# Queries and keys of a second attention, transposed in blocks by VectorE and moved through DRAM, with projections four units ahead

## The chip, the cores and the metric

The kernel runs on one core of a Trainium2 chip. The core has a matrix engine (TensorE, PE in the profile), a vector engine (VectorE, DVE), a scalar engine (ScalarE, ACT), a general engine (GpSimd, POOL) and a queue engine that only issues transfers (SyncE, SP). On-chip data lies in SBUF, 128 partitions wide; products land in PSUM. Transfers run on 16 DMA engines. The metric is the device time of one execution in microseconds, the median over runs.

## The reference

All numbers are float32. Eight sequences of 128 tokens and 512 channels pass through two residual blocks:

```
x = x + attention1(x @ cond_w[adapter])          # 32 heads of 16, causal
h = attention2(x, cached keys and values)        # 32 query heads and 8 key heads of 128
x = x + h @ kernel + bias + LoRA(h)
```

The second attention is where the change lies:

```
q = rope(rmsnorm(x @ Wq.T))                      # 32 heads of 128
k = rope(rmsnorm(x @ Wk.T)); v = x @ Wv.T        # 8 heads of 128, each serves 4 query heads
keys = concat(k_cache[block_table], k)           # 512 cached positions and 128 own
vals = concat(v_cache[block_table], v)
scores = q . keys / sqrt(128), masked by length
h = softmax(scores) . vals, then @ Wo.T
```

## The kernel before

**Units and pairs.** The second attention is cut into 64 units, each one key head g and one sequence b: 128 queries of four heads against 640 keys. Two units of the same sequence and neighbouring key heads are a pair, since one row of the gathered cache holds both heads. The order is written out by hand (a manual schedule): each engine executes its instructions in program order.

**One iteration u** of the loop over units does, on TensorE: the scores of unit u, head by head (L889 against the 512 cached keys, L896 against the 128 own keys), with the query projection of unit u+1 between the heads (L177, qp); the key and value projection of u+1 (L217, kvp); the weighted values of unit u-1 (L963); the transposes of the queries of u+1 (`queries`, L254); the output projection of u-1 (L982, yp); and the transpose of the own keys of u+1 (`own_keys`, L271). ScalarE copies both transposes out of PSUM (L256, L273). A float32 product is two weight loads and two product instructions, so each line counts twice in the profile; a transpose is one.

**Softmax.** VectorE adds mask and scores, scales and takes the maximum in one instruction for each head (L902), ScalarE takes the exponential (L912) and divides (L880, after a reciprocal on VectorE, L879). The probabilities are transposed in 32 x 32 blocks by VectorE (`turn`, L883, into `flips`, of which there is one buffer) and sixteen DMAs of 80 KB each (L936) put the blocks in place, from `flips` to `pT`. The product with the values of an iteration later reads `pT`.

**Cached keys.** From unit 4 on, they are transposed the same way: `turn_keys` (L840, four block transposes for each pair) writes `flk`, and `move_keys` (L853) issues sixteen DMAs for each pair, eight in each of two iterations, from `flk` to `kT`. `pair_keys` calls these at the third head of an iteration. For units 0 to 3 TensorE transposes them (`keys`, L263).

**Projections.** `q_turn` multiplies the projected queries with tables of cosine and sine, weighted by the norm's weights (VectorE, L200 to L202), and GpSimd adds the halves (L203). The tables `ca` and `sa` lie in SBUF for the whole kernel. `kv_turn` does the same for the keys (L232 to L235), `norms` takes the reciprocal roots (GpSimd, L244) and scales the keys (L247).

**Buffers and queues.** Scores have two PSUM tiles (`p_sc`), projections and outputs two (`p_mm`), transposes and kvp two (`p_tp`). SBUF tiles of 2 KB per partition come from a ring `tile_a` of twelve slots, which the gathered weights of the first attention (cw) and the LoRA weights (la, lb, las, lbs, gs) share. SP issues nearly all DMAs in program order[...]. GpSimd issues the gathers (kg, vg, cw).

**The first attention** runs before, in 17 steps k of half a sequence; `gather_w`, `condition` (L514), `merge_loads` (L425 to L433) and `merge_gates` (L447) lie in it.

Of the kernel before, what the change touches and what calls it, by code (L numbers as in the profile page):

```python
# [41 lines left out]
def block_kernel(  # L42
# [47 lines left out]
    def tile_a(shape, name):  # L90
        return both.tile(shape, F32, tag="a", name=name, bufs=12)

# [16 lines left out]

    ca = [one([P, B, D2], F32, f"ca_{n}") for n in range(2)]  # L110
    sa = [one([P, B, D2], F32, f"sa_{n}") for n in range(2)]
    bias = one([P, DM], F32, "bias")
# [8 lines left out]

    oT_kept = one([P, REP, S], F32, "oT_kept")

    weights = {}
# [60 lines left out]
    def q_turn(u):  # L185

        b = units[u][1]
        s = st[u]
        qp = s["qp"]

        def table(t, cols):
            return t[:, b, cols].unsqueeze(1).to_broadcast([P, REP, cols.stop - cols.start])

        s["ss"] = both.tile([P, REP + 1], F32, tag="ss", name=f"ss_{u}")
        sq = tile_a([P, REP, D2], f"sq_{u}")
        qa = s["qa"] = tile_a([P, REP, D2], f"qa_{u}")
        qb = tile_a([P, REP, D2], f"qb_{u}")

        def turn():
            nc.vector.tensor_tensor(qa[:], qp[:], table(ca[0], slice(0, D2)), ALU.mult)  # L200
            nc.vector.tensor_tensor(qb[:, :, lo], qp[:, :, hi], table(sa[0], lo), ALU.mult)
            nc.vector.tensor_tensor(qb[:, :, hi], qp[:, :, lo], table(sa[0], hi), ALU.mult)  # L202
            nc.gpsimd.tensor_tensor(qa[:], qa[:], qb[:], ALU.add)  # L203
            nc.scalar.activation(sq[:], qp[:], AF.Square)

        def squares():
            nc.vector.tensor_reduce(s["ss"][:, :REP], sq[:], AX.X, ALU.add)

        return turn, squares
# [11 lines left out]
    def kv_turn(u):  # L221

        b = units[u][1]
        s = st[u]
        kp, ss = s["kp"], s["ss"]
        junk = both.tile([P, D2], F32, tag="junk", name=f"junk_{u}", bufs=1)
        nc.scalar.activation(junk[:], kp[:, :D2], AF.Square, accum_out=ss[:, REP:])
        vo = both.tile([P, D2], F32, tag="vo", name=f"vo_{u}", bufs=3)
        nc.scalar.copy(vo[:], kp[:, D2:])
        ka = both.tile([P, D2], F32, tag="ka", name=f"ka_{u}")  # L230
        kb = both.tile([P, D2], F32, tag="kb", name=f"kb_{u}")
        nc.vector.tensor_tensor(ka[:], kp[:, :D2], ca[1][:, b, :], ALU.mult)  # L232
        nc.vector.tensor_tensor(kb[:, lo], kp[:, hi], sa[1][:, b, lo], ALU.mult)
        nc.vector.tensor_tensor(kb[:, hi], kp[:, lo], sa[1][:, b, hi], ALU.mult)
        nc.gpsimd.tensor_tensor(ka[:], ka[:], kb[:], ALU.add)  # L235
        s |= {"ka": ka, "vo": vo}

    def norms(u):
        s = st[u]
        ss, ka = s["ss"], s["ka"]  # L240

        nc.vector.tensor_scalar(ss[:], ss[:], 1.0 / D2, EPS, ALU.mult, ALU.add)  # L242
        rs = both.tile([P, REP + 1], F32, tag="rs", name=f"rs_{u}")
        nc.gpsimd.tensor_tensor(rs[:], ss[:], minus_half[:], ALU.pow)  # L244
        nq = both.tile([P, REP], F32, tag="nq", name=f"nq_{u}", bufs=3)
        nc.vector.tensor_scalar(nq[:], rs[:, :REP], -SCALE2, None, ALU.mult)
        nc.vector.tensor_scalar(ka[:], ka[:], rs[:, REP:], None, ALU.mult)  # L247
        s["nq"] = nq

    def queries(u):  # L250
        s = st[u]
        tp = p_tp.tile([P, REP, S], F32, tag="tp", name=f"qTp_{u}")
        for r in range(REP):
            nc.tensor.transpose(tp[:, r, :], s["qa"][:, r, :], ident[:])  # L254
        s["qT"] = tile_a([P, REP, S], f"qT_{u}")
        nc.scalar.copy(s["qT"][:], tp[:])  # L256

    def keys(u):
# [6 lines left out]
        nc.scalar.copy(kT[:].rearrange("p k j -> p (k j)"), tp[:].rearrange("p c k -> p (c k)"))  # L265
        s["kT"] = kT[:]

    def own_keys(u):
        s = st[u]
        tp = p_tp.tile([P, S], F32, tag="tp", name=f"kTp_{u}")  # L270
        nc.tensor.transpose(tp[:], s["ka"][:], ident[:])  # L271
        s["kTo"] = both.tile([P, S], F32, tag="kTo", name=f"kTo_{u}")
        nc.scalar.copy(s["kTo"][:], tp[:])  # L273


    with (
# [68 lines left out]
        nc.vector.tensor_copy(row_f[:], row[:])  # L345
        ahead = both.tile([P, 4, P], I32, tag="a", name="ahead", bufs=12)
        nc.gpsimd.iota(ahead[:], pattern=[[-32, 4], [1, P]], base=0, channel_multiplier=0)
# [40 lines left out]
        def angles():  # L388
# [19 lines left out]
            return (fr, trig["sin"]), (kf, trig["cos"])  # L408

        def tables(n):  # L410
            for here, there in ((lo, hi), (hi, lo)):
                w_here = wn[n][:, here].unsqueeze(1).to_broadcast([P, B, HALF])
                w_there = wn[n][:, there].unsqueeze(1).to_broadcast([P, B, HALF])
                nc.gpsimd.tensor_tensor(ca[n][:, :, here], trig["cos"], w_here, ALU.mult)
                nc.gpsimd.tensor_tensor(sa[n][:, :, here], trig["sin"], w_there, ALU.mult)
            nc.gpsimd.tensor_scalar(sa[n][:, :, lo], sa[n][:, :, lo], -1.0, None, ALU.mult)

        merge = {}

        def merge_loads():  # L420
# [7 lines left out]
            for key, src in (("las", lora_as), ("lbs", lora_bs)):  # L428
                merge[key] = tile_a([RANK, DM], key)
                nc.sync.dma_start(out=merge[key][:], in_=src)  # L430
# [7 lines left out]
        def merge_gates():  # L438
# [4 lines left out]
            )  # L443
            gs = [tile_a([P, 2, B * RANK], f"gs_{n}") for n in range(2)]
            merge["gs"] = [gs[c // 2][:, c % 2, :] for c in range(4)]
# [255 lines left out]
        for k in range(2 * B + 1):  # L701
# [45 lines left out]
            else:  # L747
# [36 lines left out]
                elif b == 2:  # L784
                    tables(1)
                    nc.gpsimd.memset(minus_half[:], -0.5)
                elif b == 3:
# [45 lines left out]

    def turn_keys(n):


        flk = p2.tile([P, 4, NBLK, 2, 32], F32, tag="flk", name=f"flk_{n}", bufs=1)
        for h, half in enumerate(pairs[n]["kg"]):
            for m in range(2):
                nc.vector.transpose(  # L840
                    flk[:, :, 2 * h : 2 * h + 2, m, :].rearrange("p b c i -> p c b i"),
                    half[:, :, m, :],
                )
        pairs[n]["flk"] = flk
        kT = p2.tile([P, NBLK, 4, 2, 32], F32, tag="kT2", name=f"kT2_{n}")
        pairs[n]["kT"] = kT
        for m in range(2):
            st[2 * n + m]["kT"] = kT[:, :, :, m, :].rearrange("p c a i -> p (c a) i")

    def move_keys(n, a):  # L850

        for b in range(4):
            nc.sync.dma_start(  # L853
                out=pairs[n]["kT"][32 * b : 32 * b + 32, :, a].rearrange("p c m i -> p c (m i)"),
                in_=pairs[n]["flk"][32 * a : 32 * a + 32, b].rearrange("p c m i -> p c (m i)"),
            )

    def pair_keys(u):

        if u == 2:  # L860
            turn_keys(u)
        if 1 < u < N - 2:
            for a in range(u % 2 * 2, u % 2 * 2 + 2):
                move_keys(u // 2 + 1, a)

    def scores(u, between, after):
# [20 lines left out]
        for r in range(REP):  # L887
            sc = p_sc.tile([P, 1024], F32, tag="sc", name=f"sc_{u}_{r}")
            nc.tensor.matmul(  # L889
                sc[:, : NBLK * P].rearrange("p (k j) -> p k j", j=32),  # L890
                s["qT"][:, r, :],
                s["kT"],
# [3 lines left out]
            nc.tensor.matmul(  # L896
                sc[:, NBLK * P : NK], s["qT"][:, r, :], s["kTo"][:], start=True, stop=True
            )
# [153 lines left out]
    for u in range(N + 1):  # L1052


        now, nxt, last = u < N, u + 1 < N, 1 <= u <= N

        def between(r):
            if nxt:
                for c in ((), (0,), (1,), (2, 3))[r]:
                    q_matmul(u + 1, c)  # L1060
                if r == REP - 1:
                    after[:] = q_turn(u + 1)

        after = [lambda: None] * 2
        if now:
            scores(u, between, after)
        if nxt:
            for c in range(KC):
                kv_matmul(u + 1, c)
            kv_turn(u + 1)  # L1070
            after[1]()
# [7 lines left out]
        if u == 0:  # L1079
            x1_last = out_proj_last()  # L1080
        if nxt:
            norms(u + 1)
            queries(u + 1)
            for v in {0: (1,), 1: (2, 3)}.get(u, ()):
                keys(v)
            if u > 2 and u % 2 and u // 2 + 2 < N // 2:
                turn_keys(u // 2 + 2)

            if u < 2:
                gather(u + 1, "kg")  # L1090
            elif u % 2 == 0:
                gather(u // 2 + 2, "kg")
            if u % 2:
                gather(u // 2 + 1, "vg")
        if u == N:
# [5 lines left out]
        if u == N - 1:  # L1101
            flips_last(u, (2, 3))
        if u == 0:
            flip_last(x1_last)
        if nxt:
            own_keys(u + 1)
        if u == 0:
            load_wo(1)

        for n in range(2):  # L1110
            g = (u + 1 - n) // (2 * B) * 2 + 2 + n
            if (u + 1 - n) % (2 * B) == 2 * B - 2 and g < NKV:
                load_qkv(g)
# [88 lines left out]
```

## Time and profile before

| | |
|---|---|
| median of 3 runs | 1414.28 us (1413.05 to 1415.44) |
| profiled execution | 1423.96 us, span 1421.1 us |
| clock of TensorE granted | 0.997 of full speed |
| first attention | 0 to about 220 us |
| one unit of the second attention | 17.8 us |
| DMA moved | 180.26 MB, mean 127 GB/s |

In lines of the profile a group shows its line of code, its engine, what it writes and reads, how often, then busy time in all, mean duration of one in ns, and after the last bar the time the engine idled before it and for whom. In lines of the timeline the first column is the start and the second the duration in us; in brackets stands the idle time before. In the chain of waits a piece is start, duration and what ran. The main groups of the second attention beside the ones shown in the prediction:

| line | what | count | mean ns |
|---|---|---|---|
| L889 | scores, 512 keys | 512 | 593 |
| L896 | scores, own keys | 512 | 275 |
| L254 | transposes of queries | 256 | 273 |
| L271 | transposes of own keys | 64 | 273 |
| L902 | mask, scale, maximum | 256 | 884 |
| L883 | block transposes of probabilities, 640 columns | 252 | 808 |
| L840 | block transposes of cached keys, 256 columns | 120 | 413 |
| L207 | sum of squares, 512 values to 4 | 64 | 665 |
| L627 | sums in the first attention, 1024 values to 8 | 32 | 1200 |

These durations include the pipeline's length: one product ends after the next has begun, so they add up to more than the time that passes.

### The profile page before, as it was taken

The numbers are of one execution on the slowest core, as the hardware profiler recorded it, in microseconds if no ns is written. First come the engines' busy times: TensorE is split into PE (matmuls) and PEld (weight loads), VectorE is DVE, ScalarE is ACT, GpSimd is POOL, SyncE is SP. The second block draws the span as 40 slices with busy tenths as digits, with TensorE's granted clock in tenths as the row PEclk, the third lists the DMA queues.
The fourth block names the chain that finished last, engine by engine and source line by source line (L and its number), as shares of the span: only waits on it lengthen the run. The fifth ranks groups of instructions, "written<-read, shape, count | busy, mean of one in ns | idle before, by whom it ended". The sixth has DMA issues, their size and how long they took to land.

```text
span 1421.1 us, 20290 instructions
## 1 busy us (share of the span) xinstructions
PE 1391.5 (98%) x6244; PEld 898.5 (63%) x6244; DVE 931.8 (66%) x2266; ACT 655.9 (46%) x1520; POOL 568.2 (40%) x553
## 2 busy tenths in 40 slices
PE   6999989999999999999999999999999999999998
PEld 6877755566666666666666666666666665666555
DVE  5777846566666666666666666666666665666651
ACT  3555535444444444444444444444444444344431
POOL 5774342433333333333333333333333433343220
PEclk9999999999999999999999999999999999999999
DMA  6255013444444565444445654444456544444440
GB/s 198 75 164 183 31 37 104 129 117 118 119 115 119 161 193 151 119 119 119 119 119 159 196 148 119 118 119 119 121 160 192 152 117 136 131 111 112 115 111 30
DMA packets 156202, 180.26 MB, mean 127 GB/s; under 512 B 92416, under 2 KB 97792, under 8 KB 156096
## 3 DMA queue, kind: packets, MB, share of 16 engines
q1 hardware_dynamic: 140544, 134.39, 34.0%
q0 software_dynamic: 15552, 44.58, 10.8%
q8 instruction: 50, 0.82, 0.2%
q14 instruction: 56, 0.46, 0.1%
HBM read 75.83 MB, written 4.72 MB: 57 GB/s over the span
## 4 chain that ended last, share of the span: by engine, by line
PE 93%; DVE 2%; issue 2%; DMA 1%; ACT 1%; POOL 1%; SPq 1%; another core or an unknown queue 0%; DVEq 0%; POOLq 0%; ACTq 0%
PE op L963 19%; PE qp L177 15%; PE sc L889 15%; PE yp L982 15%; PE kvp L217 7%; PE sc L896 4%; PE fp L1044 2%; PE hp L514 2%; PE qTp L254 2%; PE pT1p L638 2%; PE qp L530 2%; PE att L673 2%; PE o L657 1%; PE sc L595 1%; PE kvp L545 1%
## 5 line engine op out<-in xcount | busy, mean ns | idle before, releaser
L902 DVE CUSTOM_DVE_ANT_0 pr<-sc,mask,nq 128x640 f32<-128x640 f32 x256 | 226.0, 884 | 144.2 <-PE sc L896 90.9
L912 ACT ACTIVATE pr<-pr,nm 128x640 f32<-128x640 f32 x256 | 211.8, 827 | 189.3 <-DVE nm L902 102.1
L889 PE MATMUL sc<-kT,qT 128*128 128x512 f32 x512 | 262.0, 593 | 0.0
L177 PE MATMUL qp<-wq,x1T 128*128 128x512 f32 x512 | 251.2, 593 | 0.0
L963 PE MATMUL op<-pT,vg 128*128 128x256 f32 x1024 | 242.0, 379 | 1.6 <-DMA pT<-fl 1.6
L203 POOL TENSOR_TENSOR qa<-qa,qb 128x512 f32<-128x512 f32 x64 | 81.8, 1278 | 375.2 <-DVE sums L879 375.2
L982 PE MATMUL yp<-wo,oT 128*128 128x512 f32 x504 | 229.2, 598 | 2.0 <-DVE oT L971 2.0
L963 PEld LDWEIGHTS op<-pT,vg 128*128 128x128 f32 x1024 | 193.9, 190 | 27.8 <-DVE sums L879 1.8
L880 ACT ACTIVATE pr<-pr,sums 128x640 f32<-128x640 f32 x256 | 208.4, 814 | 0.0
L883 DVE STREAM_TRANSPOSE fl<-pr 128x640 f32<-128x640 f32 x252 | 189.2, 808 | 0.0
L896 PEld LDWEIGHTS sc<-kTo,qT 128*128 128x128 f32 x512 | 96.4, 190 | 124.4 <-issue 119.2
L982 PEld LDWEIGHTS yp<-wo,oT 128*128 128x128 f32 x504 | 91.4, 191 | 95.1 <-issue 91.5
L160 POOL DMA_INDIRECT kg<-in_k_cache_dram,idx_kv x128 | 131.6, 1029 | 35.3 <-issue 34.8
L160 POOL DMA_INDIRECT vg<-in_v_cache_dram,idx_kv x128 | 128.6, 1005 | 37.8 <-issue 33.6
L889 PEld LDWEIGHTS sc<-kT,qT 128*128 128x128 f32 x512 | 87.7, 191 | 80.2 <-issue 77.8
L256 ACT COPY qT<-qTp 128x512 f32<-128x512 f32 x64 | 37.5, 586 | 205.3 <-PE qTp L254 204.7
L217 PEld LDWEIGHTS kvp<-wkv,x1T 128*128 128x128 f32 x512 | 97.3, 190 | 40.5 <-issue 30.1
L217 PE MATMUL kvp<-wkv,x1T 128*128 128x256 f32 x512 | 121.0, 379 | 0.0
L244 POOL TENSOR_TENSOR rs<-ss,minus_half 128x5 f32<-128x5 f32 x64 | 76.5, 1196 | 83.1 <-DVE ss L242 82.2
L177 PEld LDWEIGHTS qp<-wq,x1T 128*128 128x128 f32 x512 | 82.8, 191 | 31.5 <-issue 31.5
L896 PE MATMUL sc<-kTo,qT 128*128 128x128 f32 x512 | 99.2, 275 | 0.0
L273 ACT COPY kTo<-kTp 128x128 f32<-128x128 f32 x64 | 17.1, 267 | 166.4 <-issue 115.2
(155 smaller groups left out, 1701.1 us busy)
## 6 DMA issues: line engine op xcount, KB each, us to landing
pT<-fl SPq DMA_DIRECT2D x1008, 80.0 KB
kT<-flk SPq DMA_DIRECT2D x480, 32.0 KB
wq<-in_wq_dram SPq DMA_DIRECT2D x8, 1024.0 KB
wo<-in_wo_dram SPq DMA_DIRECT2D x8, 1024.0 KB
wkv<-in_wkv_dram SPq DMA_DIRECT2D x8, 512.0 KB
kg<-in_k_cache_dram,idx_kv POOLq DMA_INDIRECT x128
vg<-in_v_cache_dram,idx_kv POOLq DMA_INDIRECT x128
res<-x_kept SPq DMA_DIRECT2D x8, 256.0 KB
```

Source lines behind the costliest of these rows:

```text
L160: nc.gpsimd.indirect_dma_start(out=dst[:, c].rearrange("p n d -> p (n d)"), out_offset=None, in_=src, in_offset=bass.IndirectOffsetOnAxis( ...
L177: nc.tensor.matmul(s["qp"][:].rearrange("p h d -> p (h d)"), x1T[b][:, c, :], weights[g][0][:, c, :], start=(c == 0), stop=(c == KC - 1),)
L203: nc.gpsimd.tensor_tensor(qa[:], qa[:], qb[:], ALU.add)
L217: nc.tensor.matmul(s["kp"][:], x1T[b][:, c, :], weights[g][1][:, c, :], start=(c == 0), stop=(c == KC - 1))
L880: nc.scalar.activation(prs[r][:], prs[r][:], AF.Copy, scale=sums[:, r : r + 1])
L883: nc.vector.transpose(s["flips"][:, :, :, r, :].rearrange("p b c j -> p c b j"), prs[r][:])
L889: nc.tensor.matmul(sc[:, : NBLK * P].rearrange("p (k j) -> p k j", j=32), s["qT"][:, r, :], s["kT"], start=True, stop=True,)
L896: nc.tensor.matmul(sc[:, NBLK * P : NK], s["qT"][:, r, :], s["kTo"][:], start=True, stop=True)
L902: nc.vector.tensor_tensor_reduce(out=pr[:], in0=sc[:, :NK], in1=mask[:], scale=s["nq"][:, r : r + 1], scalar=3.0e38, op0=ALU.add, op1=ALU.min,
L912: nc.scalar.activation(pr[:], pr[:], AF.Exp, bias=nm[:, r : r + 1], scale=-1.0, accum_out=sums[:, r : r + 1],)
L963: nc.tensor.matmul(ops[h][:, : 2 * S], cached(u, "vg", c) if c < NBLK else s["vo"][:], s["pT"][:, :, c, 2 * h : 2 * h + 2, :].rearrange("p ...
L982: nc.tensor.matmul(yp[:], s["oT"][:, r, :], weights[g][2][:, r, :], start=(r == 0), stop=(r == REP - 1))
```

## The change

From unit 4 on, TensorE transposes neither queries nor own keys. `turn_ahead` block-transposes both on VectorE, the queries into `flq` and the own keys into a fifth block of `flk`. For each pair, `keys_out` writes `flk` and `flq` to DRAM in two DMAs, and an iteration later `keys_in` reads them into `kT` and `qT` in eight, with the blocks in place. One head's query matrix is then `qT[:, a, i, r, m]` at fixed r and m. To leave time for this, a unit is projected four iterations ahead rather than one; iterations 0 and 1 project the units in between. Units 1 to 3 keep the transposes on TensorE. To make room, the tables go to DRAM and are loaded for each pair (`load_tab`), `tile_a` has nine slots rather than twelve, and las, lbs and gs have tiles of their own; ka, vo and nq have more buffers.

```diff
-        return both.tile(shape, F32, tag="a", name=name, bufs=12)
+        return both.tile(shape, F32, tag="a", name=name, bufs=9)
...
-    ca = [one([P, B, D2], F32, f"ca_{n}") for n in range(2)]
-    sa = [one([P, B, D2], F32, f"sa_{n}") for n in range(2)]
+    tab_kept = dram.tile([B, P, 4, D2], F32, tag="tab", name="tab_kept")
+    tabs = {}
...
+    def load_tab(n):
+        if n < N // 2:
+            tabs[n] = both.tile([P, 4, D2], F32, tag="tab", name=f"tab_{n}")
+            nc.sync.dma_start(out=tabs[n][:], in_=tab_kept[n % B])
...
     def turn_keys(n):
-        flk = p2.tile([P, 4, NBLK, 2, 32], F32, tag="flk", name=f"flk_{n}", bufs=1)
+        flk = p2.tile([P, 4, 2, NBLK + 1, 32], F32, tag="flk", name=f"flk_{n}", bufs=1)
...
+        kT = p2.tile([P, 4, 2, NBLK + 1, 32], F32, tag="kT2", name=f"kT2_{n}")
+        pairs[n]["fl"] = [flk, p2.tile([P, 4, 32, REP, 2], F32, tag="flq", name=f"flq_{n}", bufs=1)]
+        qT = p2.tile([P, 4, 32, REP, 2], F32, tag="qT2", name=f"qT2_{n}")
+        pairs[n]["to"] = [kT, qT]
         for m in range(2):
+            s = st[2 * n + m]
+            s["kT"] = kT[:, :, m, :NBLK].rearrange("p a c i -> p c a i")
+            s["qT"] = [
+                qT[:, :, :, r].rearrange("p a i m -> p (a i) m")[:, :, m] for r in range(REP)
+            ]
+            s["kTo"] = kT[:, :, m, NBLK]
+
+    def turn_ahead(v):
+        (flk, flq), m = pairs[v // 2]["fl"], v % 2
+        nc.vector.transpose(
+            flq[:, :, :, :, m].rearrange("p b i r -> p r b i"),
+            st[v]["qa"][:].rearrange("p r d -> p (r d)"),
+        )
+        nc.vector.transpose(flk[:, :, m, NBLK], st[v]["ka"][:])
+
+    def keys_out(n):
+        pairs[n]["dr"] = []
+        for k, fl in enumerate(pairs[n]["fl"]):
+            kept = dram.tile([P, 4, 320 - 64 * k], F32, tag=f"fl{k}", name=f"kept{k}_{n}", bufs=2)
+            nc.sync.dma_start(out=kept[:], in_=fl[:].rearrange(FLAT[k]))
+            pairs[n]["dr"].append(kept)
+
+    def keys_in(n):
+        for k, to in enumerate(pairs[n]["to"]):
+            kept = pairs[n]["dr"][k][:].rearrange("(a j) b x -> j b a x", j=32)
+            for b in range(4):
+                nc.sync.dma_start(
+                    out=to[32 * b : 32 * b + 32].rearrange(FLAT[k]),
+                    in_=kept[:, b],
+                )
 
     def pair_keys(u):
         if u == 2:
-            turn_keys(u)
+            turn_keys(2)
+            turn_ahead(4)
         if 1 < u < N - 2:
-            for a in range(u % 2 * 2, u % 2 * 2 + 2):
-                move_keys(u // 2 + 1, a)
+            if u % 2 == 0:
+                turn_ahead(u + 3)
+                keys_out(u // 2 + 1)
+            else:
+                keys_in(u // 2 + 1)
...
-        now, nxt, last = u < N, u + 1 < N, 1 <= u <= N
+        now, last = u < N, 1 <= u <= N
+        ahead = {0: [1, 2, 3], 1: [4, 5]}.get(u, [u + 4] if u + 4 < N else [])
...
-        if nxt:
-            norms(u + 1)
-            queries(u + 1)
...
+        if ahead:
+            norms(ahead[0])
+        if u == 0:
+            queries(1)
+            keys(1)
+        if u == 1:
+            keys(2)
+            keys(3)
+        if u > 2 and u % 2 and u // 2 + 2 < N // 2:
+            turn_keys(u // 2 + 2)
+            turn_ahead(u + 3)
...
         if u == 0:
+            project(2)
             flip_last(x1_last)
-        if nxt:
-            own_keys(u + 1)
-        if u == 0:
+            own_keys(1)
+            norms(2)
+            project(3)
+            queries(2)
+            own_keys(2)
+            norms(3)
+            load_tab(2)
+            load_tab(3)
             load_wo(1)
+        elif u == 1:
+            queries(3)
+            own_keys(3)
+            project(5)
+            norms(5)
+        if u % 2:
+            load_tab((u + 7) // 2)
 
         for n in range(2):
-            g = (u + 1 - n) // (2 * B) * 2 + 2 + n
-            if (u + 1 - n) % (2 * B) == 2 * B - 2 and g < NKV:
+            g = (u + 4 - n) // (2 * B) * 2 + 2 + n
+            if (u + 4 - n) % (2 * B) == 2 * B - 2 and g < NKV:
                 load_qkv(g)
```

## The prediction

> **What bounds the kernel.** I read the engine table first, then the chain of waits, then one unit's pieces of it.
>
> ```profile
> PE 1391.5 (98%) x6244; PEld 898.5 (63%) x6244; DVE 931.8 (66%) x2266; ACT 655.9 (46%) x1520; POOL 568.2 (40%) x553
> PE 93%; DVE 2%; issue 2%; DMA 1%; ACT 1%; POOL 1%; SPq 1%; another core or an unknown queue 0%; DVEq 0%; POOLq 0%; ACTq 0%
> 309.67 0.44 PE qTp L254 x4
> 310.11 3.44 PE yp L982 x8
> 313.55 0.11 PE kTp L271
> 313.65 0.86 PE sc L889 x2
> 314.51 0.22 PE sc L896 x2
> 314.74 0.86 PE sc L889 x2
> ```
>
> TensorE works without a gap, and the chain is its own instruction stream: columns are start, duration, line. A unit takes 17.78 us (kTp at 313.55, again at 331.33). The pieces show the pace, not the pipelined ends: a product of 512 columns holds the engine for 0.43 us, one of 128 for 0.11, that is 0.84 ns a column. So an instruction taken from TensorE is time, if nothing else then ends last.
>
> **What leaves TensorE.** The change drops L254 (four transposes, 0.44 us) and L271 (one, 0.11) for units 4 to 63: 60 x 0.55 = **-33 us**. ScalarE loses their two copies (586 and 267 ns), which were not in the chain.
>
> **The new layout of the queries.** qT was contiguous. Now one head's query is read from [a, i, r, m] with r and m innermost: 8 floats, 32 bytes, from one column to the next. It is the stationary operand. Weight loads overlap products (PEld), so a slower load costs only where the product before it is short. Per head the order is load, product of 512, twice, then load, product of 128, twice. A contiguous load is 128 columns, 0.11 us at that pace, and just fits behind a product of 128. Strided loads behind such a product: the second L896 of each head (4), and the first L889 of head 1, which has no qp between. Five per unit; the others hide behind 0.43 us.
>
> No load in the trace has such a stride. The nearest rows are two VectorE reductions of the same 128 values, one read in runs of 16, one at 128 bytes a step:
>
> ```profile
> L334 DVE TENSOR_REDUCE eye_f<-ident 128x32 f32<-128x128 f32 x1 | 0.4, 361 | 0.0
> L318 DVE TENSOR_REDUCE odd<-ident 128x2 f32<-128x128 f32 x1 | 0.3, 286 | 0.4 <-POOL ident masks.py:199 0.4
> ```
>
> The step adds 75 ns over 128 values (L334 also writes 30 more results, which may be part of it). Against the contiguous rate of L207 and L627, (1200 - 665) ns for 512 values, 128 values would be some 264 ns, and 97 is added. [...] By the rows, 0.09: 60 x 5 x 0.09 = **+27 us**. [...] A gain is excluded, since the contiguous load is hidden. I take 27.
>
> The moving operands keep runs of 32 floats, as kT had at 593 ns a product like any contiguous one: nothing.
>
> **VectorE.** turn_ahead adds two transposes a unit. By L883 (640 in steps of 0.75 us) 512 columns are 0.60 and 128 are 0.17: 0.8 us, if writes at 32 bytes are no slower; 1.1 by the reading rate above. In even units they stand before the fourth L902, where VectorE idles 0.97 us: hidden. In odd units they stand behind turn_keys:
>
> ```profile
> 828.35 0.34 DVE L247 TENSOR_SCALAR ka<-ka,rs 128x128 f32<-128x128 f32 x1
> 828.74 1.42 DVE L840 STREAM_TRANSPOSE flk<-kg 128x256 f32<-128x256 f32 x4
> 830.26 0.69 DVE L989 TENSOR_TENSOR y<-yp,y 128x512 f32<-128x512 f32 x1
> 830.87 0.55 DVE L874 TENSOR_SCALAR mask<-place,lens_f 128x640 f32<-128x640 f32 x1
> 831.56 0.88 DVE L902 CUSTOM_DVE_ANT_0 pr<-sc,mask,nq 128x640 f32<-128x640 f32 x1
> ```
>
> Behind them wait y, the mask and the first L902, and for its end waits TensorE: scores have two PSUM buffers, so head 2 needs head 0's freed. Today it is free at 832.44 and wanted at 833.19. After: L840 ends at 830.16, both transposes at 830.9, y and mask take 1.3, L902 ends near 833.05; TensorE, rid of 0.55, wants it at 832.63. It stalls 0.5 us, once a pair, 29 pairs: 14.5 us. But the loads delay TensorE too, three of the five before head 2 (0.27): 0.22 remains, **+6 us**.
>
> **The last units.** Projections run four units ahead, so iterations 60 to 62 have none; before, only 63. Without 5.1 us of qp and kvp the values (L963) come sooner than their probabilities:
>
> ```profile
> 1374.22 10.25 SPq L936 DMA_DIRECT2D pT<-fl  x16
> 1386.44 1.97 PE L963 MATMUL op<-pT,vg 128*128 128x256 f32 x8 [1.57 <-DMA pT<-fl]
> ```
>
> Sixteen issues take 10.25 us and the wait ends 1.97 after them: 12.2 from the transposed probabilities to use. Today 63 waits 1.57. In a full unit the transposes end about 12.2 us after the first L889 and the values start 9.5 into the next unit, leaving some 2.5 us. Scores alone take 4.6. Running 60 to 63 by this: waits of 2.4, 1.7 (an FFN tail lies in it), 0 and 4.2 = 8.3, less 1.57: **+7 us**. The projections themselves are moved to iterations 0 and 1, not saved; each brings its turn (VectorE 2.9 us, POOL's L203, L235 and L244, 2.9 us) in the same order among itself, under 5.1 us of its own products. At the start TensorE waits 1.06 us for own_keys(1) today; there a projection stands before each of queries(2) and own_keys(2), so I put no gain and no loss (1 us either way). The load of the next wq and wkv moves three units earlier with them, still behind pT's issues at the end of an iteration, two iterations before its first use as before.
>
> **Transfers.** Per pair sixteen kT<-flk of 32 KB (0.5 MB) become two writes and eight reads, 1.18 MB each way, plus a table load of 256 KB. pT's thirty-two stay. SP's issues fall from 48 to 43 a pair; the same eight-issue slot (5.2 to 6.8 us, L853) takes the reads. The stretches 804 to 832 us show the DMA engines at 0.36 to 0.83, 247 GB/s at 0.83; 6.3 MB in 34.5 us is 180 GB/s, so they fit. Reads issued at 817 to 823 land near 826, wanted at 829.6: hidden. The cover goes where SP issues weights just before them: wq and wkv (1.5 MB, 6 us) three times, wo (1 MB) three times. I count 3 x 1 to 2.5 and 3 x 0 to 0.7: **+5 us** (0 to 10). The write to DRAM must land before its reads issue; a whole unit lies between. keys_out adds a wait of SP for turn_ahead at the third head; behind it on SP stand this unit's pT, whose own transposes come later on the same VectorE, so nobody waits longer. The table load waits for a kv_turn of the same iteration, long over by then; q_turn reads it three iterations later.
>
> **The first attention.** Nine tile_a slots instead of twelve: lb_1 now reuses a slot of cw_7, so it waits for condition(7), which ends at 156; las waited for that before (issued at 155.41). Behind it on SP stand lb_2, lb_3, w_eff, las, lbs and gc, 1.75 MB, and VectorE's gs (L447, at 161.57) needs gc, now near 165. VectorE stalls and the copies L644 and sums behind it come late: **+3 us** (0 to 4). tab_kept (2 MB) holds SP near 93 us, where nothing behind it is due soon: 0; with no cover, its 9 us. In unit 2 two turn_aheads more precede L902 of head 3; TensorE waits there 2.0 us for oT already, 2 x 0.8 comes on top: **+1.5 us**.
>
> **Sum.** -33 + 27 + 6 + 7 + 5 + 3 + 1.5 = +16.5 us. The profiled execution took 1424.0 (span 1421.1), 10 more than the median 1414.3; so 1440 there and **1431** in the runs, slower by 1.2%. Its own range is 1418 to 1450.
>
> **Rivals.**
>
> *The strided load is free* (decides if the load stays below 0.11 us). Then the stall of VectorE is whole: -33 + 14.5 + 7 + 5 + 3 + 1.5 = -2: **1412**. With the other costs at their lower ends (0.25 a pair, 4 in the tail, no load collisions, no gc) it is -21: 1393. For it: fp32 runs at half the rate a 2-byte load shows (L583's loads 95 ns against L530's 192), so there may be room. Against it: the reductions[...].
>
> [...]
>
> *The transfers end last*: doubled bytes put the keys' reads or pT 1 us late in every pair, since pT has only 2.5 us to spare and fl is one buffer that waits for its reads. On top of the forecast 30 us: **1461**. For it: 1.3 MB of pT follow 1.2 MB of keys in the same queue. Against: the busy shares.
>
> **Chances.** Forecast 0.50, load free 0.30[...], transfers 0.12. Changes under 0.2% (2.8 us) can't be told from none. Of the free load two thirds are faster by more, the rest within or above; of the forecast a tenth falls low. Faster 0.26, same 0.09, slower 0.65. The range 1395 to 1464 leaves out [...]the best of the free load.
>
> **What would show it.** PEld's rows for L889 and L896 (191 and 190 ns now) near 280 if the load pays, unchanged if not; the chain's L896 pairs at 0.31 instead of 0.22; L902 of head 0 releasing TensorE at odd-to-even seams; waits on pT in the last three units; no wait on kT or qT reads but after weights. The forecast is wrong if L896 keeps 0.22, or if waits on transfers exceed 20 us in all.

## The result

The changed kernel takes **1453.22 us** (median of 6 runs, 1450.07 to 1453.96), the kernel before 1414.86 us on the same chip (6 runs, 1413.05 to 1416.27). The ratio is **1.0269** (95% interval 1.0256 to 1.0283): slower by 38 us. The forecast was slower by 16.5: the sign and the places are right, the size is not.

The profile of the changed kernel, by its engine table, the first line of its chain of waits and three of its groups, and below them the two load groups of the kernel before:

```profile
PE 1407.8 (97%) x5944; PEld 985.4 (68%) x5944; DVE 992.2 (68%) x2386; ACT 603.1 (42%) x1400; POOL 555.5 (38%) x553
PE 85%; DMA 4%; DVE 4%; SPq 3%; ACT 1%; issue 1%; POOL 1%; DVEq 0%; ACTq 0%; POOLq 0%
L938 PE MATMUL sc<-kT,qT 128*128 128x512 f32 x512 | 276.8, 622 | 13.4 <-DMA pT<-fl 6.9
L938 PEld LDWEIGHTS sc<-kT,qT 128*128 128x128 f32 x512 | 151.3, 314 | 89.6 <-issue 49.8
L945 PEld LDWEIGHTS sc<-kT,qT 128*128 128x128 f32 x480 | 150.3, 313 | 55.3
```

```profile
L889 PEld LDWEIGHTS sc<-kT,qT 128*128 128x128 f32 x512 | 87.7, 191 | 80.2 <-issue 77.8
L896 PEld LDWEIGHTS sc<-kTo,qT 128*128 128x128 f32 x512 | 96.4, 190 | 124.4 <-issue 119.2
```

L938 and L945 are the old L889 and L896, the scores. TensorE is busy for 97% of the span, with 300 instructions fewer and for 16 us longer; its share of the chain has fallen from 93 to 85%. The loads of its stationary operand show the main reason: 314 and 313 ns each, where they took 191 and 190. One unit's start in the chain of waits (start, duration, what ran):

```profile
840.47 0.86 PE sc L938 x2
841.33 0.35 PE sc L945 x2
841.67 0.99 PE sc L938 x2
842.66 0.34 PE sc L945 x2
843.00 0.86 PE qp L183 x2
843.86 0.86 PE sc L938 x2
844.72 0.34 PE sc L945 x2
```

A pair of 128 columns took 0.22 us before and takes 0.34; head 1's pair of 512 took 0.86 and takes 0.99, head 0's still 0.86. These are the five places that the prediction named, and no others. A unit now pays 4 x 0.12 + 0.13 = 0.61 us to save 0.55.

The second cost is at the seam from an odd to an even unit. The timeline there (start, duration, engine, line; idle time before in brackets):

```profile
820.83 1.41 DVE L862 STREAM_TRANSPOSE flk<-kg 128x256 f32<-128x256 f32 x4
822.17 1.06 DVE L881 STREAM_TRANSPOSE flq<-qa 128x512 f32<-128x512 f32 x1
823.09 0.26 DVE L885 STREAM_TRANSPOSE flk<-ka 128x128 f32<-128x128 f32 x1
823.28 0.64 DVE L1042 TENSOR_TENSOR y<-yp,y 128x512 f32<-128x512 f32 x1
823.86 0.65 DVE L923 TENSOR_SCALAR mask<-place,lens_f 128x640 f32<-128x640 f32 x1
824.66 0.88 DVE L955 CUSTOM_DVE_ANT_0 pr<-sc,mask,nq 128x640 f32<-128x640 f32 x1
825.60 0.55 PEld L938 LDWEIGHTS sc<-kT,qT 128*128 128x128 f32 x2 [1.00 <-DVE nm L955]
825.60 1.25 PE L938 MATMUL sc<-kT,qT 128*128 128x512 f32 x2 [0.17 <-DVE nm L955]
```

VectorE comes to the first L955 only after both transposes, as forecast, and head 2's product waits for it. The bracket on PE alone (0.17) hides most of the cost: the load of that product waited too (1.00), so here it doesn't lie under an earlier product, and the pair takes 1.25.

Taking the time from the start of one unit's values to the next (L963, now L1016), units 17 to 47 took 17.79 us each before; now even ones take 17.87 and most odd ones 18.44. The differences of these intervals account for the 31 us between the two spans:

| where | predicted | measured |
|---|---|---|
| transposes gone | -33 | -33 (60 x 0.55) |
| exposed loads | +27 | +38 (17.87 - 17.79 + 0.55 = 0.63 a unit) |
| seam | +6 (29 pairs x 0.22) | +9 (16 pairs x 0.57, units 17 to 47 only) |
| last units | +7 | +10 |
| weights ahead of keys and queries | +5 | +6 (units 11, 21, 27, 43) |
| start, units 0 to 2 | +4.5 | +2 |
| sum | +16.5 | +32 |

The medians differ by 38 us, the spans by 31. The other 7 are not placed: the profiled execution of the kernel before took 10 us more than its median, that of the changed kernel only 1. One thing that differs between the two profiles is a wait in the first attention near 187 us (for L644, 3.60 us before; for L656, as the line is now, 0.44). Of the eleven other profiles of this document nine have this wait and two have not; which the median executions have isn't shown.

### The profile page after: what moved, and what is told of

Read it like the earlier page. It is cut to its first block, busy times and chain, and to the rows that moved or that the text cites. A ratio compares the mean times of both kernels' runs of the same rounds, so it can differ in the third digit from the quotient of the medians.

```text
span 1452.2 us, 19400 instructions
## 1 busy us (share of the span) xinstructions
PE 1407.8 (97%) x5944; PEld 985.4 (68%) x5944; DVE 992.2 (68%) x2386; ACT 603.1 (42%) x1400; POOL 555.5 (38%) x553
## 4 chain that ended last, share of the span: by engine, by line
PE 85%; DMA 4%; DVE 4%; SPq 3%; ACT 1%; issue 1%; POOL 1%; DVEq 0%; ACTq 0%; POOLq 0%
PE op L1016 17%; PE sc L938 15%; PE yp L1035 13%; PE qp L183 13%; PE kvp L223 7%; PE sc L945 5%; PE fp L1097 2%; PE hp L526 2%; SPq L989 2%; DMA kT<-kept 2%; PE pT1p L650 2%; PE att L685 2%; PE qp L542 1%; DVE pr L955 1%; PE o L669 1%
## 5 line engine op out<-in xcount | busy, mean ns | idle before, releaser
L955 DVE CUSTOM_DVE_ANT_0 pr<-sc,mask,nq 128x640 f32<-128x640 f32 x256 | 224.4, 883 | 116.7 <-PE sc L945 108.1
L938 PE MATMUL sc<-kT,qT 128*128 128x512 f32 x512 | 276.8, 622 | 13.4 <-DMA pT<-fl 6.9
L1016 PE MATMUL op<-pT,vg 128*128 128x256 f32 x1024 | 243.4, 381 | 2.7 <-DVE sums L928 2.7
L1016 PEld LDWEIGHTS op<-pT,vg 128*128 128x128 f32 x1024 | 194.7, 191 | 29.5 <-DVE sums L928 3.2
L938 PEld LDWEIGHTS sc<-kT,qT 128*128 128x128 f32 x512 | 151.3, 314 | 89.6 <-issue 49.8
L945 PEld LDWEIGHTS sc<-kT,qT 128*128 128x128 f32 x480 | 150.3, 313 | 55.3
L166 POOL DMA_INDIRECT vg<-in_v_cache_dram,idx_kv x128 | 123.9, 968 | 40.6 <-issue 30.0
L166 POOL DMA_INDIRECT kg<-in_k_cache_dram,idx_kv x128 | 124.2, 970 | 35.3 <-issue 34.5
L945 PE MATMUL sc<-kT,qT 128*128 128x128 f32 x480 | 121.7, 335 | 0.0
L183 PEld LDWEIGHTS qp<-wq,x1T 128*128 128x128 f32 x512 | 86.3, 196 | 34.4 <-issue 34.4
L641 POOL TENSOR_TENSOR pr<-pr,sums 128x1024 f32<-128x1024 f32 x32 | 60.0, 1898 | 70.1 <-DVE sums L640 58.5
L630 ACT ACTIVATE pr<-sc,nm 128x128 f32<-128x128 f32 x256 | 67.9, 416 | 32.9 <-DVE nm L616 32.9
```

Of the source, the lines that this page charges most:

```text
L166: nc.gpsimd.indirect_dma_start(out=dst[:, c].rearrange("p n d -> p (n d)"), out_offset=None, in_=src, in_offset=bass.IndirectOffsetOnAxis( ...
L183: nc.tensor.matmul(s["qp"][:].rearrange("p h d -> p (h d)"), x1T[b][:, c, :], weights[g][0][:, c, :], start=(c == 0), stop=(c == KC - 1),)
L938: nc.tensor.matmul(sc[:, : NBLK * P].rearrange("p (c a j) -> p c a j", c=NBLK, j=32), s["qT"][r], s["kT"], start=True, stop=True,)
L945: nc.tensor.matmul(sc[:, NBLK * P : NK].rearrange("p (a j) -> p a j", j=32), s["qT"][r], s["kTo"], start=True, stop=True,)
L955: nc.vector.tensor_tensor_reduce(out=pr[:], in0=sc[:, :NK], in1=mask[:], scale=s["nq"][:, r : r + 1], scalar=3.0e38, op0=ALU.add, op1=ALU.min,
L1016: nc.tensor.matmul(ops[h][:, : 2 * S], cached(u, "vg", c) if c < NBLK else s["vo"][:], s["pT"][:, :, c, 2 * h : 2 * h + 2, :].rearrange("p ...
```

## The experiments

Each ratio is to the kernel before, run alongside on the same chip. The medians of before were 1420.28 (first three kernels below and the repeat), 1421.49 (the next four) and 1415.45 (the last two).

**The stationary operand read in a row.** One edit: the same products read 128 consecutive floats of qT. These belong to other queries, so what is left out is the right query for each score; the work and the transfers are the same in number and size.

```diff
-                qT[:, :, :, r].rearrange("p a i m -> p (a i) m")[:, :, m] for r in range(REP)
+                qT[:].rearrange("p a i r m -> p (a i r m)")[:, (2 * r + m) * S : (2 * r + m + 1) * S]
+                for r in range(REP)
```

> The changed kernel with one edit: each head's stationary operand is read as 128 consecutive floats of qT instead of every eighth one. The bytes are others, so the output is not the reference's; work, transfers and waits are the same in number and size. Theory (the step of the stationary operand is what costs): weight loads of L938 and L945 fall from 313 ns to 190, the pairs of L945 in the chain from 0.34 to 0.22 us, a unit by 0.65 us where VectorE does not hold it; VectorE's stall at the seam of two units grows by some 0.27 us a pair since TensorE comes there earlier. 60 x 0.65 = 39 less, 16 x 0.27 = 4 more: 1418 us. Rival (the loads only look long, and transfers or VectorE set the pace): 1445 to 1453 us, loads at 190 ns all the same.

Ratio 1.0067 (1.005 to 1.0083), 1430.46 us. The weight-load group:

```profile
L939 PEld LDWEIGHTS sc<-kT,qT 128*128 128x128 f32 x512 | 90.2, 192 | 118.3 <-issue 108.0 <-DVE nm L956 10.3
```

The load is back at 192 ns; units take 17.25 (even) and 18.06 (odd), against 17.87 and 18.44. So 0.62 us of an even unit is the stride of this one operand. The time fell by 0.0202 of before, 29 us, not the whole 37: the odd units keep a longer seam stall (0.81), as the prediction's rival had it, since TensorE now comes to head 2 earlier (16 x 0.24 = 4 us), and units 11, 27 and 43, at loads of weights, lose 4 us more than they did (some 3.4 of it, by the estimate of 1.7 given below for the last units, in two stretches of slow products: in the timeline a pair of 512 takes 2.05 us at 460.69 and 1.92 at 1030.84, where the median is 1.02).

**The stride put into the kernel before.** ScalarE writes its copy of the queries interleaved, with the four heads side by side (4 floats from column to column) or two (2 floats). Transfers and VectorE's work stay as they are; the diff is that of 4 floats, without the two lines that read qT.

```diff
-        s["qT"] = tile_a([P, REP, S], f"qT_{u}")
-        nc.scalar.copy(s["qT"][:], tp[:])
+        qT = tile_a([P, S, REP], f"qT_{u}")
+        nc.scalar.copy(qT[:].rearrange("p s r -> p r s"), tp[:])
+        s["qT"] = [qT[:, :, r] for r in range(REP)]
```

> The kernel before with one edit: the copy of the transposed queries writes them interleaved by head, so the stationary operand of the scores steps by 4 floats (16 bytes) from column to column; nothing else changes. Theory [...]: loads 313 ns, six of them a unit behind a product of 128 columns (one more than in the changed kernel, behind the transpose of the own keys): 64 x 6 x 0.123 = 47 us more, 1462 us. Rival [...]: loads 190 ns, 1415 us. Rival (cost grows with the step): loads near 250 ns, about 1438 us.

> As before_step4, with heads interleaved in twos: a step of 2 floats (8 bytes)[...]. Theory[...]: loads 190 ns, 1415 us. Rival (any step costs): loads 313 ns, 1462 us. Rival (cost grows with the bytes spanned): loads near 220 ns, about 1427 us.

One run each: 1462.47 us (+42, where 47 was expected) at 4 floats, 1424.72 (+4) at 2. The load groups, first at 4, then at 2:

```profile
L890 PEld LDWEIGHTS sc<-kT,qT 128*128 128x128 f32 x512 | 149.9, 316 | 64.5 <-issue 48.3 <-DMA pT<-fl 0.2
```

```profile
L892 PEld LDWEIGHTS sc<-kT,qT 128*128 128x128 f32 x512 | 90.6, 196 | 79.4 <-issue 77.1 <-DVE nm L905 2.0 <-DMA pT<-fl 0.2
```

And the chain of the kernel at 4 floats, at the start of a unit:

```profile
832.80 0.11 PE kTp L272
832.91 0.98 PE sc L890 x2
833.88 0.34 PE sc L897 x2
834.23 0.98 PE sc L890 x2
```

At 4 floats the load costs what it costs at 8 (316 and 314 ns), at 2 the step is nearly free (196). Why the cost sets in between 2 and 4 floats isn't shown. Six loads a unit are exposed in this kernel, since a transpose of 128 columns (L272) stands before head 0, and a unit grew by 0.71 (18.50 against 17.79): 6 x 0.12. ScalarE's copy (L256) grows too, from 586 ns to 1077 at 4 floats and 618 at 2, but it isn't the cause: TensorE waits for it for less than 2 us in the whole profile at 4. The stride alone, in a kernel with no other part of the change, costs as much as the whole change does.

**The kernel before, profiled again.** 

> The kernel before, unchanged, profiled once more: its first profile (1424.0 us) lies 10 us above its median, the changed kernel's (1454.0) only 1. Theory (the first profile held disturbances of its own): the span now is near 1412 us, and units 49 to 58 take less time than in the first profile. Rival (profiling slows this kernel): again near 1421.

1421.58 us, span 1419.7, beside a median of 1420.28 on that chip. The two profiles agree (the first had a span of 1421.1), so the theory of a disturbed first profile falls; and this one lies 1 us above its median, not 10, so profiling doesn't slow this kernel by 10 either. Medians differ by 0.5% between chips. Where the first 10 us come from stays open; they are no property that a changed kernel would share. Only ratios on one chip are used for times here.

**Queries at a step of 2 floats in the changed kernel.** The two units of a pair stay interleaved, the heads do not. The price is three more transfers a pair (13 instead of 10), since the four blocks of a head have to come together on the way through DRAM; these edits of `turn_ahead`, `keys_out` and `keys_in` are left out below.

```diff
-        pairs[n]["fl"] = [flk, p2.tile([P, 4, 32, REP, 2], F32, tag="flq", name=f"flq_{n}", bufs=1)]
-        qT = p2.tile([P, 4, 32, REP, 2], F32, tag="qT2", name=f"qT2_{n}")
+        pairs[n]["fl"] = [flk, p2.tile([P, 4, REP, 32, 2], F32, tag="flq", name=f"flq_{n}", bufs=1)]
+        qT = p2.tile([P, REP, 4, 32, 2], F32, tag="qT2", name=f"qT2_{n}")
...
-                qT[:, :, :, r].rearrange("p a i m -> p (a i) m")[:, :, m] for r in range(REP)
+                qT[:, r].rearrange("p a i m -> p (a i) m")[:, :, m] for r in range(REP)
```

> The changed kernel with another layout of the queries: qT is [r, a, i, m], so the stationary operand steps by 2 floats instead of 8. The blocks are put in place on the way out, in four writes of 128 KB with runs of 256 bytes, and read back in runs of 4 KB; thirteen transfers a pair instead of ten. Theory ([...]VectorE's transpose L881, 1.06 us, gets cheaper with the same step): loads near 196 ns, L881 near 0.65 us, even units 17.3 us (from 17.9), odd units 17.7 (from 18.4): some 35 us less than the changed kernel, ratio to the kernel before 1.003. Rival (runs of 256 bytes to DRAM are too slow): waits of TensorE on kT or qT in every pair, ratio above 1.015. If L881 keeps 1.06 us, odd units stay at 18.05 as in flat_read, ratio 1.007.

Ratio 1.0078 (1.0061 to 1.0095), where 1.003 was expected. The load group, the block transposes of the queries, and two of TensorE's waits (for what, us in all, times, longest):

```profile
L946 PEld LDWEIGHTS sc<-kT,qT 128*128 128x128 f32 x512 | 93.0, 196 | 109.5 <-issue 91.2 <-DVE nm L963 18.0 <-DMA pT<-fl 0.2
L881 DVE STREAM_TRANSPOSE flq<-qa 128x512 f32<-128x512 f32 x60 | 40.8, 679 | 0.0
```

```profile
PE op L1024 <- DMA pT<-fl: 10.2, 5, 2.8
PE sc L946 <- DMA pT<-fl: 7.0, 5, 1.7
```

The same layout cures two things: the load, and VectorE's own transpose, 679 ns instead of 1078 (its writes step by 8 bytes, not 32). Even units take 17.29: the 0.5 us that the change was to bring is there. That the kernel is still slower is down to the rest. Waits on transfers, 7 us before this edit in these two rows, are now 17. A unit that is 0.6 us shorter leaves the transfers less time: the kernel that reads in a row, with as short units and the ten transfers a pair of the changed kernel, has 14 in its rows.

**The seam.** The odd unit's transposes go from behind `turn_keys` to head 1 of the next iteration, where VectorE has time.

```diff
             turn_keys(u // 2 + 2)
-            turn_ahead(u + 3)
...
+            if r == 1 and 2 < u < N - 2 and u % 2 == 0:
+                turn_ahead(u + 2)
             if r == 2:
                 pair_keys(u)
```

> The changed kernel with the turn_ahead of odd iterations moved from behind turn_keys to the second head of the next even iteration, where VectorE idles about 1.1 us before L955. Theory (the two transposes behind turn_keys hold up head 0's L955 and so TensorE at the seam, 0.56 us a pair from unit 17 to 47): odd units 17.9 us instead of 18.4, 16 x 0.56 = 9 us less, ratio 1.021. Rival (they only shift the stall, to the heads 1 and 2 of the even unit): ratio within 0.002 of 1.027.

Ratio 1.0209 (1.0191 to 1.0227), lower by 0.0060, 8.5 us. In its chain of waits, both of two neighbouring units begin like this, and neither has a longer pair at head 2 (the last line):

```profile
825.24 0.86 PE sc L938 x2
826.10 0.34 PE sc L945 x2
826.45 0.99 PE sc L938 x2
827.43 0.34 PE sc L945 x2
827.78 0.86 PE qp L183 x2
828.64 0.86 PE sc L938 x2
```

The units from 18 to 47 take 17.87, even and odd, but for 27 and 43 behind weights. The +9 of the table is shown.

**The last units.** Projections of units 62 and 63 are held back, so that iterations 59 and 61 have one (`queries` and `own_keys` of 63 on TensorE again).

```diff
-        ahead = {0: [1, 2, 3], 1: [4, 5]}.get(u, [u + 4] if u + 4 < N else [])
+        ahead = {0: [1, 2, 3], 1: [4, 5], N - 6: [], N - 5: [N - 2], N - 3: [N - 1]}.get(
+            u, [u + 4] if u + 4 < N - 2 else []
+        )
...
+        if u == N - 3:
+            queries(N - 1)
+            own_keys(N - 1)
```

> The changed kernel with the last projections spread: iterations 58, 60 and 62 make none, since FFN work lies ahead of them, and units 62 and 63 are projected in iterations 59 and 61; unit 63's queries and own keys go through TensorE. Theory (without a projection and without FFN work TensorE waits for pT: 5.0, 0.5, 2.5 and 1.7 us in the last four units): these waits go but for the 1.57 us that the kernel before has too, 8 to 9 us less, ratio 1.021. Rival (the waits come from queue and transfers alone): ratio 1.026 or more.

Ratio 1.0305 (1.0282 to 1.0328): no gain, rather a loss. The theory falls. Units 57 to 63 together take 132.9 us against 130.9. The timeline of the changed kernel without this edit, where TensorE waits in its last units:

```profile
1368.29 5.40 PE L1035 MATMUL yp<-wo,oT 128*128 128x512 f32 x8 [2.02 <-DVE oT L1024]
...
1380.01 1.97 PE L1016 MATMUL op<-pT,vg 128*128 128x256 f32 x8 [0.67 <-DVE sums L928]
...
1404.23 3.70 PE L1035 MATMUL yp<-wo,oT 128*128 128x512 f32 x8 [1.68 <-DVE oT L1024]
...
1415.67 2.42 PE L1016 MATMUL op<-pT,vg 128*128 128x256 f32 x8 [2.08 <-DVE sums L928]
```

Two of these waits are for VectorE (3.7 us), which the prediction had not worked out: without projections the values end before ScalarE's divisions, and VectorE's copies oT stand in its order behind the transposes that need them. The two of L1016 (2.75 us) are for pT, as forecast, whatever name stands in the bracket: the last transfer of pT lands at 1379.44 and 1415.36, and the products, which read pT and not sums, start 0.6 and 0.3 us later. A further part of the +10 is the clock. The first yp takes 5.40 us and the other 3.70 for the same eight products: the granted clock was 0.50 for 3.4 us from 1369.2, and again from 1417.0, each time shortly behind one of these waits (2.02 and 2.08 us), and 1.00 before and after. That is some 1.7 us each, an estimate from 5.40 - 3.70, and the kernel before has no such stretch in its last units.

With the edit, TensorE waits for oT (5.5 us), pT (2.6) and the own keys of 63 (1.9) instead. How far another order on VectorE would shorten these waits is open.

**All three together.** 

> q_step2, seam and tail together. If the three costs add, 35 + 5 + 9 us less than the changed kernel: ratio to the kernel before 0.993, 1404 us where the kernel before takes 1415. The steady unit would take 17.3 us in even and odd. Rival (what is taken from TensorE comes back as waits for pT or keys, since units get shorter while the transfers do not): ratio 1.00 to 1.01.

Ratio 1.006 (1.0039 to 1.0081), where 0.993 was expected. Undisturbed units take 17.29, even and odd, and yet the kernel is not faster than before, as the rival in the expectation had it. With the last-units edit taken out again:

> Queries at a step of 2 floats, and the transposes of the odd units at head 1 of the next even iteration; the last units as in the changed kernel. If the two repairs add up, this is q_step2 less the 0.35 us that its odd units in 17 to 47 are longer than its even ones, 15 pairs, some 5 us: near 1.004 of before. Units of 17.29 us, even and odd alike. If the last-units edit was what kept all_three above before, it comes out below all_three (1.006) by what that edit cost alone, 0.010 of before, so near 0.997.

Ratio 1.005 (1.0037 to 1.0063), 1422.69 us. The two repairs add up as expected of them (q_step2 less some 4 us); taking the last-units edit out brings nothing that can be told from none, so its harm does not add. What keeps this kernel above before is read from its windows (stretch, its length, busy time of PE, PEld, DVE, ACT and POOL with counts, granted clock, DMA busy share, GB/s): unit 10 (weights issued at its end), 11 and 12.

```profile
428.00:446.00 18.00, 18.00 (x64) 11.36 (x63) 12.29 (x34) 7.62 (x17) 6.84 (x8) 1.00 0.63 163
446.00:465.00 19.00, 17.35 (x61) 10.54 (x60) 13.60 (x37) 8.12 (x17) 6.81 (x7) 1.00 0.97 252
465.00:483.00 18.00, 17.89 (x63) 10.99 (x62) 11.94 (x33) 8.08 (x18) 7.27 (x8) 1.00 0.81 243
```

And in the kernel before, a unit with no load of weights ahead of it, then the unit behind the first such load (issued at 478.9):

```profile
448.00:466.00 18.00, 18.00 (x68) 11.41 (x67) 11.86 (x31) 8.63 (x19) 7.02 (x8) 1.00 0.43 115
483.80:501.60 17.80, 17.80 (x67) 11.24 (x66) 11.67 (x31) 8.44 (x19) 7.12 (x8) 1.00 0.65 174
```

The DMA engines are nearly full (0.97) for the unit after this load, where they were at 0.65 before. Units 4 to 48 lose 11 us over their 17.29, nearly all of it at or just behind loads of wq, wkv and wo. Whether it is order or amount was the last question (the second edit, which reads the gates and small LoRA weights ahead of la and lb, is left out):

```diff
-        nc.sync.dma_start(out=wkv[:], in_=wkv2[:, g, :].rearrange("(c p) e -> p c e", p=P))
         weights[g] = [wq, wkv]
+        held.append((wkv, g))
...
                 pair_keys(u)
+                load_held()
```

> step2_seam with two changes of the order in which SP issues transfers and nothing else: of each weights load of 1.5 MB the 0.5 MB of keys and values go behind the key transfers of the next iteration's third head, and the gates and small LoRA weights are read ahead of la and lb. If the shorter units lose some 14 us to weights that stand ahead of the transfers of keys and probabilities, a third to a half of it, 5 to 7 us, comes back, and 3 us in the first attention: 8 to 10 us less than step2_seam, near 0.997 of before. If those waits come from something else, the time is step2_seam's within 2 us.

Ratio 1.0035 (1.0022 to 1.0049), 1419.78 us: 2 to 3 us less, with the intervals overlapping. The collisions did not shrink, they moved: unit 11 went from 19.18 to 17.29, unit 12 from 17.62 to 18.41, units 16 and 17 from 18.09 and 19.16 to 19.47 and 20.04 (some 1.8 of the last by an estimate: the granted clock was 0.91 over the 20 us from 547); 12 us in all. So this order was not the cause. That the amount is, fits the share of this kernel's DMA engines, 0.98 and 0.90 in the two stretches after the load, but no run with fewer bytes shows it. The gates read early did their part: TensorE's longest wait in the first attention for VectorE's pT fell from 3.92 us (near 174) to 0.7, as the 3 us expected of it; whether the ratio's gain is this or chance can't be told.

## Why the prediction was off

**What bounds the kernel: right.** TensorE was busy for 96 to 98% of the span in all twelve profiles, and an instruction taken out was time: with the operand in a row units fall from 17.79 to 17.25, by 0.54 of the 0.55.

**The strided load: the step that failed.** The prediction said "By the rows, 0.09: 60 x 5 x 0.09 = +27 us". The five places were right; the 0.09, taken from VectorE's reductions, was not. The load grew by 0.123 us (191 to 314), and 0.61 to 0.63 a unit appear, +38 in place of 27. With that term the exchange turns round: -33 + 27 was a gain of 6, -33 + 38 is a loss. Of the 22 us between forecast and measurement, 11 are this term, 3 each the seam and the last units, 1 the transfers, less 2 at the start; 7 are those between spans and medians, which stay open. A row of another engine gave the order of TensorE's price and not its size. The signs it named came, too large: loads of 314 ns for "near 280", pairs of 0.34 for 0.31. The rival "strided load is free" falls.

**The seam: right in mechanism, short in size.** L881 takes 1.08 us and L885 0.27, against the 0.60 and 0.17 taken; the prediction held the other end (1.1 together) but didn't take it. And the load that waits with its product was missing from the sum: 0.57 a pair instead of 0.22. It struck 16 pairs, not 29: units 3 to 16 and 48 to 58 show no such difference between odd and even. In the trace, y of the first key head isn't VectorE's work (at 421.36 the mask follows L885 at once), and from unit 48 on 4.3 us of FFN products stand before the scores. That +6 and +9 lie so near is luck: 2.6 times the stall in about half the pairs.

**The last units: +10, not +7**, and its nearness is luck in part: of the 8.3 us of waits on pT that the prediction forecast 2.75 came, and VectorE's order (3.7) and the granted clock of 0.50 (some 3.4, the estimate above), which it hadn't seen, made up the rest.

**Transfers: right.** +6 against +5, and where it was put. The profile names pT<-fl for the four waits of L938 (6.9 us), but these products read kT and qT. In all four the product starts 0.1 to 0.4 us after the last qT read has landed (458.70 for the first, which starts at 458.83), while the last pT transfers issued behind it are still under way, and in three of them the reads were issued right behind wq and wkv. The rival "transfers end last" falls for the changed kernel, and becomes true in part once its units are made shorter.

**The first attention:** gc landed at 166.3 (165 forecast) and VectorE's gs waited 4.68 us for it; TensorE's product of it came 3.2 us late (+3 forecast). In this profile the shorter wait near 187 us gives that back: the product behind it starts at 186.53, before at 186.74.

**The subtraction from the profile.** The prediction took the distance from the profiled execution to the median as a constant 10. The changed kernel's profile lay within 1 us of its median; the sum of effects belongs onto the median itself as a ratio. In this case the forecast is 1431 either way.

## What to carry to other kernels

Before moving a transpose off TensorE, ask in what step its successor will be read as the stationary operand: of the steps measured here with fp32, 2 floats was nearly free (196 ns a load, 191 in a row), and 4 and 8 (316 and 314 ns) cost 0.71 and 0.61 us a unit, more than the transposes' 0.55. A slower load showed here only behind a short product or a wait (head 1's pair of 512 at 0.99, head 0's still at 0.86), so count these places, and measure the load in the old kernel with one changed layout. And an engine's time that is freed shortens the period for every queue: check the DMA share at the loads of weights, which come in a few units of sixteen, not the mean (with both repairs 0.97 just behind such a load, 0.61 three units later). Read the name of a wait against the operands: the four waits put down to pT<-fl (6.9 us) ended when the reads of qT had landed.

## What the hardware showed unexpectedly

- A weight load of 128 fp32 columns took 190 to 192 ns contiguous, 196 to 198 at a step of 2 floats, 309 to 316 at 4 and 313 to 314 at 8: no step measured lies between the two levels.
- A block transpose of 128 x 512 on VectorE took 1078 ns with writes 32 bytes apart and 679 with writes 8 bytes apart. ScalarE's copy of 128 x 512 shows the same: 586 ns in a row, 618 with writes 8 bytes apart, 1077 at 16.
- The product that waited for its PSUM buffer at 825.60 in the changed kernel had its load waiting with it (idle 1.00 us, then 1.25 for the pair instead of 0.86), so this stall cost more than the 0.17 on the product's own row.
- The granted clock of TensorE was 0.50 for 3.4 us from 1369.2 and 1417.0 and for 6.8 us from 277.0 in the changed kernel, and for 3.4 us from 188.2 and 273.5 in the kernel before, each time late in a wait of TensorE or shortly behind one (2.00 to 3.60 us). Behind another wait (2.92 us from 455.9) it stayed at 1.00; what sets it off isn't shown. A stretch of 3.4 us costs some 1.7 us, an estimate from the 5.40 and 3.70 us of yp.
